# A bitwise search on VectorE: the count's start as a constant with one more column of gates, and a choice with one scalar and one tensor operand

## The chip, the cores and the metric

The kernel runs on one core of a Trainium2 chip. The metric is the device time of one execution in microseconds; the time before is the median of three runs. The profile is one further execution, recorded instruction by instruction. The engines are called PE (TensorE; PEld are its weight loads), DVE (VectorE), ACT (ScalarE), POOL (GpSimd) and SP (the queue that issues most transfers).

## What is computed

A transformer block with a mixture of experts, in float32, on 16 sequences of 256 tokens of width 256. The part that matters here is the routing, in which every expert takes the same number of tokens:

```python
shift = silu(t) @ W_ada.T + b_ada
h = _ln(x, ln1_g, ln1_b) + shift
# q, k, v of 16 heads of 64; layer norm on q and k; softmax attention
x = x + o @ Wout.T
tok = x.reshape(-1, d)                      # 4096 tokens
gate = softmax(tok @ Wgate.T, axis=-1)      # 8 experts
k_cap = bs // E                             # 512
vals, idx = top_k(gate.T, k_cap)            # each expert picks its 512 tokens
g = _ln(tok[idx], mlp_g, mlp_b)
y = (gelu(g @ fc1.T + b1) @ fc2.T + b2) * vals
tok = tok.at[idx].add(y)
```

## The kernel before

**Stages.** The sequences run through attention one after another, each split into steps (first norm, projections, scores, softmax, products, output projection, second norm, gates). Steps of neighbouring sequences are laid into each other. Up to line 1271 all engines follow a plan written out by hand: every step has a place (a number), the steps are sorted by place, and are issued in that order. So each engine has a fixed order of instructions, and an instruction that waits holds everything behind it on its engine. After that a loop over 15 jobs follows, in 16 slots each: matmuls of one expert, with the list, gather and transposes of the next job laid between.

**Two halves of the routing.** Each expert's 512 tokens are found in two halves of 256 (`CAPL`). The first search looks at the gates of the tokens that are ready (the others are held at -1.0 in `gate_of`), while the attention of the last sequence is still running. The second one runs inside the loop over jobs, and works on the gates that the first one left over. The jobs of the first half start as soon as their list is there.

**The first search** (`Routing`, steps placed by `SEARCH`, lines 437 to 453 and 1244) finds for every expert the bit pattern of the gate that 256 gates reach. `gT` holds the gates turned: 128 partitions of 256 gates, 16 partitions to an expert. There are 30 rounds, one bit each, and a round has four steps:

- `compare_less` (line 948) calls `compare` (898): one instruction on DVE compares 256 gates with the candidate `cand` and adds up how many reach it, starting the sum at `begin`, which is -255 on the first of an expert's 16 partitions and 0 on the others. The sum, `cnt`, comes out through a second small instruction that reads the accumulator.
- `count_over` (952): one matmul on PE adds the sums of an expert's 16 partitions, with the matrix `twice`, and leaves twice the surplus over 255 in PSUM (`pc`).
- `either` (958): two small operations on DVE make the two possible next candidates, `keep` and `drop`.
- `decide` (968): one operation on DVE makes the next candidate, the larger of `pc` and `drop`, but at most `keep`. A count enough gives `keep`, one too small gives `drop`.

After the rounds `masks` (977) marks the gates above and at the limit, and `scans`, `totals`, `place`, `turn_places`, `split` and `choose` give each chosen token its place. The lists of the jobs are then made with one-hot tiles (`onehot`, 1072) and matmuls (`list_matmul`, 1087); `gather` (1104) fetches the rows.

**The second search** takes two bits in a round, with three compares (`compare_three`, line 918), each with the candidate as its one scalar operand and without a start.

**Around the search** lie on PE the last sequence's projections (`pm`, line 631), transposes of q and k (`pq`, 673), scores (`sc`, 706), transposes of probabilities (`pp`, 742) and products (`po`, 760); on DVE their maxima (`nmax`, 713), sums of squares (`ss`, 648) and reciprocals (729); on ACT exponentials (722) and copies (640, 752, 770); on POOL powers (82) and scalings (664, 733).

**Preparation.** `make_others` (line 126), placed early in the plan, makes `high`, the first candidate, and `begin`. `gT` has one buffer in the pool `route`, which both searches use in turn; `reach`, the compares' element output that nobody reads, has two in the pool `bit`.

Of the kernel before, what the change touches and what calls it, by code (L numbers as in the profile page):

```python
# [9 lines left out]
F32 = mybir.dt.float32  # L10
I32 = mybir.dt.int32
BF16 = mybir.dt.bfloat16
AF = mybir.ActivationFunctionType
ALU = mybir.AluOpType
# [4 lines left out]
P = 128  # L19
# [13 lines left out]
CAPL = CAP // 2  # L33
# [10 lines left out]
def kernel(  # L44
# [14 lines left out]
    nc = tc.nc  # L59

    const = ctx.enter_context(tc.tile_pool(name="const", bufs=1))
    dram = ctx.enter_context(tc.tile_pool(name="dram", bufs=1, space=DRAM))
    route = ctx.enter_context(tc.tile_pool(name="route", bufs=1))
    bit = ctx.enter_context(tc.tile_pool(name="bit", bufs=2))
# [26 lines left out]
    vals = const.tile([P, E, NT, NV], BF16, name="vals")  # L91
    gate_of = const.tile([P, E, NT], F32, name="gate_of")
    high = const.tile([P, 1], I32, name="high")
    begin = const.tile([P, 1], F32, name="begin")
    first16 = const.tile([P, 1], I32, name="first16")

    def make_block():
# [28 lines left out]
    def make_others():  # L126
        nc.gpsimd.memset(gate_of, -1.0)
        nc.gpsimd.memset(high, 1 << 29)
        nc.gpsimd.iota(first16, pattern=[[0, 1]], base=0, channel_multiplier=1)
        nc.vector.tensor_scalar(first16, first16, 15, None, ALU.bitwise_and)  # L130
        nc.vector.tensor_scalar(begin, first16, 0.0, float(1 - CAPL), ALU.is_equal, ALU.mult)

    qgb = const.tile([P, 2], F32, name="qgb")
    sT = const.tile([P, DC, B], F32, name="sT")
# [341 lines left out]
    if True:  # L476
# [101 lines left out]
        class First:  # L578
# [22 lines left out]
            def evict(self):  # L601
                b = self.b
                hTs[b] = seq.tile([P, DC, N], F32, tag="hT", name=f"hT{b}")
                for c in range(DC):
                    nc.scalar.activation(
                        hTs[b][:, c, :], self.pt[:, c, :], AF.Identity,
                        bias=bias1[:, c, b : b + 1],
                        scale=vec[:, LN1_G + c : LN1_G + c + 1],
                    )
# [260 lines left out]
        class Routing:  # L870
# [11 lines left out]
                    nc.tensor.transpose(self.pt[:, r, :], gr[:, r, :], ident)  # L882

            def evict(self):
                self.gT = route.tile([P, 2 * P], F32, tag="gT", name="gT")
                pt = self.pt.rearrange("p r k -> p (r k)")
                if self.before is None:
                    nc.vector.tensor_copy(self.gT, pt)
                else:
                    nc.vector.scalar_tensor_tensor(  # L890
                        self.gT, self.before.chosen, -4.0, pt, ALU.mult, ALU.add
                    )
                self.cand = high

            def compare(self, n, start=None):
                reach = bit.tile([P, 2 * P], BF16, tag="reach", name="reach")
                self.cnt = bit.tile([P, 1], BF16, tag="cnt", name="cnt")  # L900
                nc.vector.tensor_scalar(
                    reach, self.gT, self.cand.bitcast(F32), start, ALU.is_ge, ALU.add,
                    accum_out=self.cnt,
                )


            def candidates(self, n):
# [10 lines left out]
            def compare_three(self, n):  # L918
                self.cnt = bit.tile([P, 3], BF16, tag="cnt3", name="cnt3")
                for k in range(3):  # L920
                    reach = bit.tile([P, 2 * P], BF16, tag="reach", name="reach")
                    nc.vector.tensor_scalar(
                        reach, self.gT, self.three[:, k : k + 1].bitcast(F32), None,
                        ALU.is_ge, ALU.add, accum_out=self.cnt[:, k : k + 1],
                    )

# [20 lines left out]

            def compare_less(self, n):

                self.compare(n, begin)  # L950

            def count_over(self, n):

# [14 lines left out]
            def decide(self, n):  # L968
                keep, drop = (new.bitcast(F32) for new in self.next)
                self.cand = bit.tile([P, 1], I32, tag="cand", name="cand")  # L970
                nc.vector.tensor_scalar(
                    self.cand.bitcast(F32), self.pc, drop, keep, ALU.max, ALU.min,
                )

# [257 lines left out]
        for k, f in enumerate((  # L1232
            make_block, make_twice, make_lanes, partial(make_vals, 0), partial(make_vals, 1),
            make_others,
        )):
            at([(4 + k / 8) * PERIOD], f)
# [156 lines left out]
```

## Time and profile before

| what | us |
|---|---|
| median of three runs (1182.08 to 1182.89) | 1182.83 |
| the profiled execution, its own time | 1182.07 |
| its span in the trace | 1180.30 |
| first search, from the first compare to the masks | 863.4 to 904.9 |
| first list's gather issued | 917.6 |
| busy over the span: PE, DVE, ACT, POOL | 1155.7, 755.3, 632.7, 593.2 |

All stamps are microseconds from the start of the span. A row of the groups view names line, engine, operation, what is written and read, the shapes and the count; behind the bar the busy time of all of them, then the mean duration of one in ns, then the engine's idle time before them and who ended it. The rows of the timeline give start, duration, engine, line and operation; in square brackets how long the engine had been idle and on whom it waited. "issue" is a wait with no cause that the profile shows. Operations of DVE that follow each other overlap a little, so the distance from one start to the next can be shorter than the duration. An operation with `accum_out` shows as `TENSOR_SCALAR_CACHE_REDUCE` and is followed by a `DVE_READ_ACCUMULATOR`.

### The profile page before, as it was taken

The page shows a single profiled execution, that of the slowest core. Times are in us where ns is not written, and L with a number is a line of the kernel's source. Part 1 is how long each engine was busy: PE and PEld are TensorE (multiplying, and loading weights), DVE is VectorE, ACT ScalarE, POOL GpSimd, SP SyncE. Part 2 cuts the span into 40 slices and gives each one's busy share as a digit, 9 for nine tenths or more (in the row PEclk, how much of TensorE's full clock was granted, in tenths as well). Part 3 has the DMA queues.
Part 4 walks back from the last instruction along what each step waited for, and adds up shares of the span by engine and source line. Part 5 has one row for each costly group of instructions (what it writes and reads, how often), then busy time and mean ns, then how long its engine had stood idle before and what let it go on. Part 6 is the DMA issues. An engine that isn't in the chain of part 4 may idle for free. (4 is left out here: it accounts for less than half of the span.)

```text
span 1180.3 us, 19683 instructions
## 1 busy us (share of the span) xinstructions
PE 1155.7 (98%) x6823; PEld 816.9 (69%) x6823; DVE 755.3 (64%) x2295; ACT 632.7 (54%) x1729; POOL 593.2 (50%) x821
## 2 busy tenths in 40 slices
PE   9999999999999999999999999999988899999996
PEld 5666666666666666666666666677745788888885
DVE  7656566657666566666666666665588578755540
ACT  4856656556565656565655565656466333233331
POOL 5846554556555555555555545464572233233332
PEclk9999999999999999999999999999999999999999
DMA  6000000000000000000000000000020465666661
GB/s 198 1 1 6 9 14 19 10 19 15 13 23 6 23 11 19 10 23 6 23 10 27 10 10 18 10 10 14 20 88 1 123 182 184 187 188 188 186 186 21
DMA packets 46739, 62.41 MB, mean 53 GB/s; under 512 B 3888, under 2 KB 39984, under 8 KB 46640
## 3 DMA queue, kind: packets, MB, share of 16 engines
q1 hardware_dynamic: 36864, 49.03, 12.5%
q0 software_dynamic: 6144, 8.39, 3.9%
q10 hardware_dynamic: 3632, 3.74, 1.0%
q8 instruction: 54, 0.88, 0.3%
q14 instruction: 45, 0.37, 0.1%
HBM read 48.56 MB, written 12.58 MB: 52 GB/s over the span
## 5 line engine op out<-in xcount | busy, mean ns | idle before, releaser
L631 PE MATMUL pm<-wq,hT 128*128 128x512 f32 x768 | 360.5, 599 | 1.2 <-ACT v L640 1.2
L733 POOL TENSOR_SCALAR pr<-pr,sums 128x256 f32<-128x256 f32 x512 | 236.5, 480 | 201.7 <-DVE sums L729 166.6
L722 ACT ACTIVATE pr<-sc,nmax 128x256 f32<-128x256 f32 x512 | 236.3, 477 | 125.1 <-DVE nmax L713 105.7
L82 POOL TENSOR_TENSOR ss<-ss,neghalf 128x8 f32<-128x8 f32 x128 | 211.6, 1655 | 172.9 <-DVE ss L652 162.5
L631 PEld LDWEIGHTS pm<-wq,hT 128*128 128x128 f32 x768 | 133.4, 190 | 120.3 <-issue 108.0
L713 DVE TENSOR_REDUCE nmax<-sc 128x2 f32<-128x512 f32 x256 | 166.4, 684 | 42.9 <-PE sc L706 42.9
L648 DVE TENSOR_REDUCE ss<-sq 128x8 f32<-128x512 f32 x128 | 87.3, 682 | 102.1 <-ACT sq L644 102.0
L742 PEld LDWEIGHTS pp<-ident,pr 128*128 128x128 f32 x1024 | 119.0, 141 | 47.3 <-issue 20.8
L742 PE MATMUL pp<-ident,pr 128*128 128x128 f32 x1024 | 138.4, 273 | 0.0
L644 ACT ACTIVATE sq<-pm 128x512 f32<-128x512 f32 x128 | 77.1, 603 | 99.0 <-PE pm L631 98.6
L706 PE MATMUL sc<-kT,qT 64*128 64x256 f32 x1024 | 129.7, 390 | 0.0
L760 PE MATMUL po<-prT,v 128*64 128x256 f32 x1024 | 124.6, 385 | 0.0
L706 PEld LDWEIGHTS sc<-kT,qT 64*128 64x128 f32 x1024 | 93.7, 186 | 38.2 <-issue 26.1
L784 PE MATMUL pw<-wo,oT 128*128 128x256 f32 x512 | 118.0, 383 | 0.0
L1135 PE MATMUL ph<-xT,w 128*128 128x256 f32 x512 | 117.8, 383 | 0.0
L1151 PE MATMUL py<-w,hid 128*128 128x256 f32 x512 | 116.3, 380 | 0.0
L1168 POOL DMA_INDIRECT out<-y,idx x32 | 51.2, 1601 | 123.9 <-DVE y L1162 70.7
L784 PEld LDWEIGHTS pw<-wo,oT 128*128 128x128 f32 x512 | 96.8, 192 | 18.9 <-issue 6.7
L722 ACT ACTIVATION_READ_ACCUMULATOR pr<-sc,nmax 128x1 f32 x512 | 106.3, 208 | 0.0
L1142 ACT ACTIVATE hid<-ph,vec 128x256 f32<-128x256 f32 x128 | 60.0, 473 | 83.5 <-PE ph L1135 78.3
L1151 PEld LDWEIGHTS py<-w,hid 128*128 128x128 f32 x512 | 95.6, 190 | 12.8
L1135 PEld LDWEIGHTS ph<-xT,w 128*128 128x128 f32 x512 | 95.3, 190 | 13.2 <-ACT xT L1123 0.4
(136 smaller groups left out, 1303.8 us busy)
## 6 DMA issues: line engine op xcount, KB each, us to landing
w<-in_fc2T SPq DMA_DIRECT2D x16, 1024.0 KB, 5.7
w<-in_fc1T SPq DMA_DIRECT2D x16, 1024.0 KB, 8.6
out<-tok SPq DMA_DIRECT2D x32, 128.0 KB, 1.7
xn_dram<-tn SPq DMA_DIRECT2D x32, 128.0 KB, 1.7
xs<-in_x SPq DMA_DIRECT2D x12, 256.0 KB, 2.8
b<-in_b2s SPq DMA_DIRECT2D x16, 128.0 KB, 8.7
wq<-in_wqkvT SPq DMA_DIRECT2D x3, 512.0 KB, 6.7
wq<-in_wqkvT ACTq DMA_DIRECT2D x3, 512.0 KB, 6.5
```

The costliest lines, as they stand in the source:

```text
L82: nc.gpsimd.tensor_tensor(dst, src, neghalf[:, : src.shape[1]], ALU.pow)
L631: nc.tensor.matmul(self.pm, hTs[self.b][:, c, bass.ts(self.t, P)], wq[:, c, bass.ts(self.g, GW)], start=(c == 0), stop=(c == DC - 1),)
L648: nc.vector.tensor_reduce(self.ss[:, 0, :], self.sq.rearrange("p (h d) -> p h d", d=HD), AX.X, ALU.add,)
L706: nc.tensor.matmul(self.sc[i, j][:, t, :], qTs[self.b][rows, hp, bass.ts(t, P)], kTs[self.b][rows, hp, :], start=True, stop=True,)
L713: nc.vector.tensor_reduce(self.nmax[i, j], self.sc[i, j], AX.X, ALU.max, negate=True)
L722: nc.scalar.activation(self.pr[i, j][:, t, :], self.sc[i, j][:, t, :], AF.Exp, bias=self.nmax[i, j][:, t : t + 1], scale=1.0, accum_out=se ...
L733: nc.gpsimd.tensor_scalar(self.pr[i, j][:, t, :], self.pr[i, j][:, t, :], self.sums[i][:, 1, j, t : t + 1], 1.0, ALU.mult, ALU.mult,)
L742: nc.tensor.transpose(self.pp[i, j][:, c, bass.ts(t, P)], self.pr[i, j][:, t, bass.ts(c, P)], ident,)
L760: nc.tensor.matmul(self.po[j * HD : (j + 1) * HD, i, :], vs[self.b][:, c, bass.ts(4 * self.d + 2 * i + j, HD)], self.prT[i, j][:, c, :], s ...
L784: nc.tensor.matmul(self.pw, oTs[self.b][:, hp, bass.ts(self.t, P)], wo[:, hp, :], start=(hp == 0), stop=(hp == HP - 1),)
L1135: nc.tensor.matmul(self.ph[f], self.w1[:, c, bass.ts(f, P)], self.xT[:, c, :], start=(c == 0), stop=(c == DC - 1),)
L1151: nc.tensor.matmul(self.py[i], self.hid[:, f, bass.ts(i, P)], self.w2[:, f, :], start=(f == 0), stop=(f == FC - 1),)
```

## The change

The column `begin` goes. Instead the tile of gates that the first search reads, `gates1`, has 257 columns, and its last one holds 3.0 on the first of an expert's 16 partitions and -1.0 on the others: a gate that always reaches the candidate, and one that never does. The sum starts at the constant -16 (`CAPL / 16`) on every partition, so that over an expert's 16 partitions it is 1 - 256 as before. `decide` takes `drop` as a scalar and `keep` as a tensor of one column. The second search uses the first 256 columns of a tile that is now one column wider, and `reach` is wider too. The order of the steps in the plan stays.

```diff
-    begin = const.tile([P, 1], F32, name="begin")
+    gates1 = route.tile([P, 2 * P + 1], F32, tag="gT", name="gates1")
...
-        nc.vector.tensor_scalar(begin, first16, 0.0, float(1 - CAPL), ALU.is_equal, ALU.mult)
+        nc.vector.tensor_scalar(
+            gates1[:, 2 * P :], first16, 0.5, 4.0, ALU.is_lt, ALU.mult
+        )
+        nc.vector.tensor_scalar_add(gates1[:, 2 * P :], gates1[:, 2 * P :], -1.0)
...
             def evict(self):
-                self.gT = route.tile([P, 2 * P], F32, tag="gT", name="gT")
                 pt = self.pt.rearrange("p r k -> p (r k)")
                 if self.before is None:
+                    self.gT = gates1[:, : 2 * P]
                     nc.vector.tensor_copy(self.gT, pt)
                 else:
+                    self.gT = route.tile([P, 2 * P + 1], F32, tag="gT", name="gT")[:, : 2 * P]
...
-            def compare(self, n, start=None):
-                reach = bit.tile([P, 2 * P], BF16, tag="reach", name="reach")
-                self.cnt = bit.tile([P, 1], BF16, tag="cnt", name="cnt")
-                nc.vector.tensor_scalar(
-                    reach, self.gT, self.cand.bitcast(F32), start, ALU.is_ge, ALU.add,
-                    accum_out=self.cnt,
-                )
...
             def compare_three(self, n):
-                    reach = bit.tile([P, 2 * P], BF16, tag="reach", name="reach")
+                    reach = bit.tile([P, 2 * P + 1], BF16, tag="reach", name="reach")
                     nc.vector.tensor_scalar(
-                        reach, self.gT, self.three[:, k : k + 1].bitcast(F32), None,
+                        reach[:, : 2 * P], self.gT, self.three[:, k : k + 1].bitcast(F32), None,
...
             def compare_less(self, n):
-                self.compare(n, begin)
+                reach = bit.tile([P, 2 * P + 1], BF16, tag="reach", name="reach")
+                self.cnt = bit.tile([P, 1], BF16, tag="cnt", name="cnt")
+                nc.vector.tensor_scalar(
+                    reach, gates1, self.cand.bitcast(F32), -CAPL / 16.0, ALU.is_ge, ALU.add,
+                    accum_out=self.cnt,
+                )
...
             def decide(self, n):
-                nc.vector.tensor_scalar(
+                nc.vector.scalar_tensor_tensor(
                     self.cand.bitcast(F32), self.pc, drop, keep, ALU.max, ALU.min,
                 )
```

## The prediction

> **What bounds the kernel now.** I read the page's busy times first, then the windows view cut at the borders of the first search, then the waits inside it, the groups by shape, and last the timeline of single rounds. The chain that ended last reaches back only over the final scatter (0.2% of the span) and helps nothing here.
>
> ```profile
> PE 1155.7 (98%) x6823; PEld 816.9 (69%) x6823; DVE 755.3 (64%) x2295; ACT 632.7 (54%) x1729; POOL 593.2 (50%) x821
> ```
> ```profile
> 862.00:905.00 43.00, 35.54 (x220) 21.47 (x222) 39.44 (x181) 29.76 (x86) 27.35 (x48) 1.00 0.03 8
> 905.00:925.00 20.00, 17.10 (x145) 13.11 (x141) 15.63 (x74) 8.61 (x25) 4.98 (x7) 0.91 0.07 21
> 925.00:1172.00 247.00, 243.96 (x1554) 213.28 (x1552) 144.45 (x778) 79.87 (x164) 80.04 (x66) 1.00 0.59 170
> ```
> The columns are length, then busy time of PE, PEld, DVE, ACT and POOL, granted clock, DMA share, GB/s. Over the whole span PE is the bound (98%). In the 43 us of the first search it is not: PE is busy 35.5, VectorE 39.4. The waits there name the cause:
>
> ```profile
> PE pc L956 <- DVE reach L901: 6.7, 10, 1.0
> ...
> PEld L956 <- DVE reach L901: 3.4, 5, 1.2
> ...
> DVE cand L971 <- PE pc L956: 0.3, 2, 0.2
> ```
> PE's order is fixed, so a count matmul that waits for VectorE's compare holds all matmuls behind it, and these belong to the last batch's attention. In the opposite direction VectorE waits hardly at all. So the search stage is set by VectorE and by the latency of the search's own loop. How the loop's latency adds up, from one round with nothing else between:
>
> ```profile
> 888.40 0.54 DVE L901 TENSOR_SCALAR_CACHE_REDUCE reach<-gT,cand,begin 128x256 bf16<-128x256 f32 x1
> ...
> 888.87 0.09 DVE L901 DVE_READ_ACCUMULATOR reach<-gT,cand,begin 128x1 bf16 x1
> ...
> 889.00 0.16 PE L956 MATMUL pc<-cnt,twice 128*128 128x1 bf16 x1 [0.39 <-DVE reach L901]
> ...
> 889.21 0.28 DVE L971 TENSOR_SCALAR cand<-pc,drop,keep 128x1 f32<-128x1 f32 x1
> ...
> 889.52 0.54 DVE L901 TENSOR_SCALAR_CACHE_REDUCE reach<-gT,cand,begin 128x256 bf16<-128x256 f32 x1
> ```
> Start to start: compare to accumulator read 0.47, to the count 0.13, to the decision 0.21, to the next compare 0.31; together 1.12 us. The search runs from 863.39 to the masks at 904.95, 41.6 us for 30 rounds: 1.12 is the round when bare, the rest are rounds into which VectorE's max, sums and scaling of attention (0.68 each) are laid. Both kinds contain one compare and one decision in sequence.
>
> **The change part by part.** The prices come from VectorE's groups by shape:
>
> ```profile
> L922 DVE TENSOR_SCALAR_CACHE_REDUCE reach<-gT,three 128x256 bf16<-128x256 f32 x45 | 19.2, 475 | 0.0
> L901 DVE TENSOR_SCALAR_CACHE_REDUCE reach<-gT,cand,begin 128x256 bf16<-128x256 f32 x29 | 15.6, 538 | 0.9
> ...
> L567 DVE TENSOR_SCALAR rs<-mv 128x1 f32<-128x1 f32 x64 | 9.8, 154 | 2.2
> L971 DVE TENSOR_SCALAR cand<-pc,drop,keep 128x1 f32<-128x1 f32 x30 | 8.3, 275 | 2.5 <-PE pc L956 0.3
> ...
> L944 DVE TENSOR_TENSOR cand<-cand,bits 128x1 int32<-128x1 int32 x13 | 2.1, 160 | 0.4
> ...
> L1004 DVE SCALAR_TENSOR_TENSOR place<-place,offset,mask 128x256 f32<-128x256 f32 x4 | 1.8, 483 | 0.1
> ...
> L1038 DVE SCALAR_TENSOR_TENSOR chosen<-places,one 128x256 f32<-128x256 f32 x1 | 0.4, 424 | 0.0
> ```
> Three pairs give one price for a per-partition scalar operand. Compare with two such (538) against one (475): 63 ns. One-column operation with two (275) against constants only (154): 60 each. Scalar-tensor-tensor with one (483) against none (424): 59.
>
> *Compare (L901).* It loses the scalar `begin` and gains a column. 475 ns is the same instruction with one scalar operand; 475 - 154 - 60 = 261 ns for 256 columns is 1.0 ns a column, so the new one is about 476, 62 ns less. No operation of 257 columns is in the trace. The cheap end is 475; at the dear end the odd width or the constant start eats the saving and it stays at 538. I take 476, because two rows (L922, and L981 at 476) carry the same form and one column is one element of a stream.
>
> *Decision (L971).* One scalar operand becomes a tensor operand. Nearest rows: tensor-tensor on one column 160, plus one scalar operand 60: 220. From L1004, 483 less 256 columns at 1.04 gives 217. The cheap end is 215, the dear end 275. I take 220: 55 ns less.
>
> The Trainium skill speaks against both. Its page "VectorE: DVE Perf Modes", section "The TRN2 errata — SBUF-src ops pay a fixed extra latency per instruction", prices an operation by where its source lies and by its columns, with no term for scalar operands, and its "Rules for kernel authors" advise lowering the number of operations, not fusing. The change keeps the number of operations in a round. By the page the sum is one cycle more per compare, an estimated 30 x 1 ns = 0.03 us lost: 1182.9. By the rows it is 30 x (62 + 55) = 3.5 us gained. The rows are three agreeing pairs from this kernel, so I go with them.
>
> *Preparation.* `begin` was one column operation of 154 ns at 282.3 us; now there are two, 0.15 us more. It hides under PE, 98% busy: VectorE has long idle spots in attention (102 us before the sums L648 alone). Bare it would cost 0.15 us.
>
> *Placement.* The order of instructions on all five engines is the same apart from that one. The build shifts every SBUF tile behind the bit pool by 64 bytes, and gives some of the small PSUM tiles another bank: in round 9 the count instead of the transposes before it waits for ACT's copy of v (done 875.50; the count ran 877.10), and in round 15 the projection behind the count waits for a copy done at 883.13 instead of the count (884.84). Both are over long before; nothing. No DMA is touched, and none is moved past.
>
> *What passes on.* A round in which VectorE is busy throughout gives up 117 ns like a bare one, unless PE's own matmuls between two counts take longer than the new round. I walked the timeline through 30 rounds, shifting each count to the later of the accumulator and the matmuls ahead of it. Eight scores (L706) between two counts take 1.16 to 1.18 us from count to count, eight transposes (L742) 1.06, four projections (L631) 1.83, sixteen products (L760) 1.97. A bare round falls to 1.00. The worst case is already late:
>
> ```profile
> 890.22 1.13 PE L706 MATMUL sc<-kT,qT 64*128 64x256 f32 x8
> ...
> 891.29 0.18 PE L956 MATMUL pc<-cnt,twice 128*128 128x1 bf16 x1
> ...
> 891.50 0.28 DVE L971 TENSOR_SCALAR cand<-pc,drop,keep 128x1 f32<-128x1 f32 x1 [0.18 <-PE pc L956]
> ```
> Lost: rounds 11 and 20 behind scores the whole 0.12 each, rounds 14 and 23 0.07 and 0.18 (where earlier gain runs into the same wall); rounds 19, 27, 28 behind eight transposes 0.17 together; rounds 16, 22, 25 behind projections and products 0.05. Sum 0.7. ACT and POOL are nearly full from 870 to 886, but their results are wanted later: POOL's scalings read at 886.7 end at 883.0. After the search the totals (906.41) stand behind sixteen products and come 0.1 late. So 3.5 - 0.7 - 0.1 = 2.7 us.
>
> The stage behind it is a chain from the search's result: places, one-hots (ACT's ten end at 916.9, and the list matmuls wait for them), list, gather at 917.6, then PE full to the end (244 of 247 us). The whole of it moves forward with the search. The profiled execution would go from 1182.07 (span 1180.30 and 1.77 around it) to 1179.4; the median of the runs, 0.76 above it, from 1182.83 to 1180.1.
>
> **The rivals.** *Scalar operands cost nothing inside the loop* (the page's view), or the 63 ns hide in the overlap of compare and accumulator read: 1182.8. Against it, masks L981 (0.48) reach their accumulator read after 0.40 us, the compare after 0.47. Chance 0.08.
>
> *Only one of the two savings comes, or PE and ACT hold more rounds than I counted*: the compare alone gives 1.5, the decision alone 1.3, half of the loss I found again 0.4: 1181.0 to 1181.9. For it speaks that 2.7 rests on margins of some 0.05 us between the loop and the matmuls. Chance 0.25.
>
> *The clock takes it back, and more.* From 914 to 917 PE is 43% busy (it waits for ACT's one-hots), and the next 3 us run at a granted clock of 0.50: sixteen projections take 5.25 us, where twelve at full clock took 2.86 (3.8 for sixteen), so the dip costs 1.4. The skill's "TensorE: Matmul & The Clock Gate", "Part 1: The HAM clock gate", says that the gate judges by a free-running window of about 3.4 us: with the search 2.7 us shorter the idle time falls elsewhere in it. One more such window takes 1.4, and from two more (2.9) on the kernel is slower; three would give 1180.1 + 4.3 = 1184.4. Against it, the gap itself is unchanged and PE has less idle time before it. Slower: chance 0.04.
>
> *The dip vanishes*: 1180.1 - 1.4 = 1178.7. Chance 0.06.
>
> **How the numbers follow.** My own case, 1180.1 within 0.5 either way, has 0.57. A measurement tells 0.2%, 2.4 us, from no change, that is below 1180.5 or above 1185.2. Three quarters of my own case and the vanished dip lie below 1180.5, and a little of the partial case: 0.43 + 0.06 + 0.04 = 0.53 faster. Slower by as much only if the clock case goes further than priced: 0.02. The rest, 0.45, is the same. The range runs from 1179.0 to 1182.0: it takes in my case and the partial one, and leaves out the vanished dip, the page's case and the clock, some 0.18.
>
> **What would show it.** Compare rows of 128x257 near 476 ns, decision rows (now scalar-tensor-tensor) near 220; bare rounds of 1.00 us; the stretch from the first compare to the masks 38.8 us instead of 41.6; PE's wait for `reach` down from 10 us in all to about 7; the gather 2.7 us earlier, and 925 to the end as long as before. It is wrong if the rows shrink and the search doesn't (then PE, ACT or POOL is the wall), if the search shrinks and the end doesn't move (the clock or the gather), or if the decision stays near 275.

## The result and the profile after

The changed kernel takes 1179.36 us (median of 13 runs, 1177.58 to 1182.5); the kernel before takes 1183.44 (13 runs, 1180.89 to 1184.55, the first three of them those that the forecast started from). The ratio of the two is 0.9971, with a 95% interval from 0.9962 to 0.998: the change gains some 3.4 us, by the interval 2.4 to 4.5. The profiled execution of the changed kernel took 1179.38 us, its span is 1177.6.

The windows view, at the same three stages as before. Columns: length, then busy time of PE, PEld, DVE, ACT and POOL, granted clock, DMA share, GB/s. The page's totals stand above it.

```profile
PE 1155.4 (98%) x6823; PEld 818.6 (70%) x6823; DVE 752.7 (64%) x2296; ACT 632.5 (54%) x1729; POOL 593.2 (50%) x821
```
```profile
862.00:902.30 40.30, 34.41 (x213) 20.67 (x212) 36.48 (x174) 29.49 (x90) 28.39 (x50) 1.00 0.07 25
902.30:922.30 20.00, 16.91 (x155) 12.84 (x154) 16.77 (x84) 9.88 (x29) 4.91 (x7) 1.00 0.07 21
922.30:1169.30 247.00, 244.24 (x1556) 213.58 (x1555) 144.63 (x778) 80.14 (x164) 80.41 (x66) 1.00 0.58 170
```
The second row of the kernel before had a granted clock of 0.91; here it is 1.00. The third row is what it was, and over the whole span PE is busy 98% as before. VectorE's groups in the search, by shape, and the waits there:

```profile
L950 DVE TENSOR_SCALAR_CACHE_REDUCE reach<-gates,cand 128x257 bf16<-128x257 f32 x29 | 14.0, 484 | 0.9
...
L974 DVE SCALAR_TENSOR_TENSOR cand<-pc,drop,keep 128x1 f32<-128x1 f32 x30 | 6.5, 216 | 3.0 <-PE pc L959 1.4
```
```profile
PE pc L959 <- DVE reach L950: 5.6, 9, 1.2
...
PEld L959 <- DVE reach L950: 1.5, 4, 0.6
DVE cand L974 <- PE pc L959: 1.4, 6, 0.3
```
The compare fell from 538 to 484 ns, the decision from 275 to 216. PE's waits for the compare (PE and PEld together) fell from 10.1 to 7.1 us, and VectorE's waits for the count rose from 0.3 to 1.4: the first comes of the gain, the second shows that PE's own matmuls now hold some of the counts back. A bare round is exactly as long as forecast, 1.00 us:

```profile
887.65 0.48 DVE L950 TENSOR_SCALAR_CACHE_REDUCE reach<-gates,cand 128x257 bf16<-128x257 f32 x1
...
888.65 0.48 DVE L950 TENSOR_SCALAR_CACHE_REDUCE reach<-gates,cand 128x257 bf16<-128x257 f32 x1
```

The two spans differ by 2.7 us, which is the number I forecast, but not by the sum that I forecast. I measured four stretches in both traces:

| stretch | before | after | difference |
|---|---|---|---|
| start of the span to the first compare | 863.39 | 864.92 | +1.53 |
| first compare to the masks | 41.56 | 39.11 | -2.45 |
| masks to the first expert matmul | 20.23 | 18.72 | -1.51 |
| first expert matmul to the end | 255.12 | 254.85 | -0.27 |

The first row has nothing to do with the change. PE's first weight loads differ already (the eight for `pa`, before and after):

```profile
5.05 1.09 PEld L512 LDWEIGHTS pa<-sT,wa 128*128 128x128 f32 x8 [0.34 <-issue]
```
```profile
4.82 1.78 PEld L517 LDWEIGHTS pa<-sT,wa 128*128 128x128 f32 x8
```
The first store of a finished token tile is then issued at 94.61 in one trace and at 96.15 in the other, and they stay 1.53 to 1.54 us apart up to 857. The 14 profiles of this study fall into two groups of seven: in one these loads take 0.97 to 1.20 us and the store is issued at 93.9 to 94.6, in the other they take 1.78 us and it is issued at 95.9 to 96.5. The changed kernel is in both (late here, early in its second profile, e0), and so are variants of the kernel before (e8 early, e9 late). The clock column reads 1.00 there in both traces, so what slows PE is not shown. The third row is the low clock of the kernel before, which the other trace does not have. So the agreement of the pair is in part luck, and the experiments below work on the second and the third row.

### The profile page after: what moved, and what is told of

Same layout as the page of the kernel before. It is cut to its first block, busy times and chain, and to the rows that moved or that the text cites. A ratio compares the mean times of both kernels' runs of the same rounds, so it can differ in the third digit from the quotient of the medians.

```text
span 1177.6 us, 19684 instructions
## 1 busy us (share of the span) xinstructions
PE 1155.4 (98%) x6823; PEld 818.6 (70%) x6823; DVE 752.7 (64%) x2296; ACT 632.5 (54%) x1729; POOL 593.2 (50%) x821
```

## The experiments

Two theories stood against each other for the part of the gain that was missing in the search (2.45 of 2.8 forecast): that PE's matmuls between two counts hold more rounds than I had counted, or that something else on VectorE became longer. For the third row the question was whether the change itself moves the clock.

**One half of the change alone.** e1 is the changed kernel with the old decision, e2 the old kernel with the new decision.

```
e1   -nc.vector.scalar_tensor_tensor(
     +nc.vector.tensor_scalar(
          self.cand.bitcast(F32), self.pc, drop, keep, ALU.max, ALU.min,
e2   the reverse, on the kernel before
```


> The new compare with the decision as before. If the search's loop sets the stage and both operations lie in it: compare rows 484 ns, decision rows 275; 30 x 0.054 = 1.6 us come off, about 0.4 of it lost again to PE and POOL, so first compare to masks 40.3 us (before 41.56, with both parts 39.11), time about 1.2 us under before. If the gain hangs on one operation alone: 39.1 here, and 41.6 in the run with the decision alone, or the other way round. If the time came from the start and the clock and not from the search: 41.6 here too.

> The new decision with the compare as before. By the theory of the loop: decision rows 217 ns, compare rows 538; 30 x 0.058 = 1.7 us come off and 0.4 are lost again: first compare to masks 40.2 us, time 1.3 us under before. By the rival, one operation alone: 41.6 or 39.1. By the rival of start and clock: 41.6.

Groups of e1, then of e2:

```profile
L950 DVE TENSOR_SCALAR_CACHE_REDUCE reach<-gates,cand 128x257 bf16<-128x257 f32 x29 | 14.0, 484 | 0.9
L974 DVE TENSOR_SCALAR cand<-pc,drop,keep 128x1 f32<-128x1 f32 x30 | 8.3, 276 | 2.7 <-PE pc L959 0.9
```
```profile
L901 DVE TENSOR_SCALAR_CACHE_REDUCE reach<-gT,cand,begin 128x256 bf16<-128x256 f32 x29 | 15.6, 538 | 0.9
L971 DVE SCALAR_TENSOR_TENSOR cand<-pc,drop,keep 128x1 f32<-128x1 f32 x30 | 6.5, 215 | 2.7 <-PE pc L956 0.7
```
The search took 40.27 us in e1 and 40.20 in e2, that is 1.29 and 1.36 less than before; together 2.65, where both at once gave 2.45. So each half gives about half, and they add up nearly. In time: e1 1182.12 (7 runs), ratio 0.9975 (0.9964 to 0.9987); e2 1181.92 (18 runs), ratio 0.9983 (0.9974 to 0.9991).

**The price of the compare's new form.** I had forecast 476 ns and 484 came. e3 lets the compare read 256 columns with the same constant start (it leaves out the column of gates that the change adds); e4 makes the tile 258 wide instead of 257, the last column a constant -1.

```
e3   -reach, gates1, self.cand.bitcast(F32), -CAPL / 16.0, ...
     +reach[:, : 2 * P], self.gT, self.cand.bitcast(F32), -CAPL / 16.0, ...
e4   -gates1 = route.tile([P, 2 * P + 1], ...)
     +gates1 = route.tile([P, 2 * P + 2], ...)      (reach and the later gT too)
     +nc.vector.memset(gates1[:, 2 * P + 1 :], -1.0)
```


> The changed kernel with the compare over 256 columns, but still with the constant start. It leaves out the extra column of gates, so every count is one lower. It asks why the compare took 484 ns where 476 were forecast. If the constant start costs it: 483. If the odd width does: 475.

> The changed kernel with 258 columns, the last one a gate of -1.0 everywhere that never reaches a candidate. If the odd width costs 8 ns: 477. If any column past 256 costs, or the constant does: 485 or a little more.

```profile
L950 DVE TENSOR_SCALAR_CACHE_REDUCE reach<-gates,cand 128x256 bf16<-128x256 f32 x29 | 13.9, 478 | 0.9
```
```profile
L951 DVE TENSOR_SCALAR_CACHE_REDUCE reach<-gates,cand 128x258 bf16<-128x258 f32 x29 | 14.0, 481 | 0.9
```
256 columns take 478, 258 take 481, 257 take 484. Against the 475 of the row that I had priced from, the constant start costs 3 ns at most, two columns more cost 3, and the odd width 4 or so on top of its column. Neither explanation alone covers the 8 ns. A bare round takes 1.00 us with each of the three widths and the search stays at 39.10 and 39.13 us, so the 8 ns are not what is missing; the one run of each took 1179.27 and 1177.2.

**The changed kernel again.**

> The changed kernel once more, to have it on the chip of the next three: 3.4 us under before (0.9971), give or take 1. Search stage (first compare to masks) 39.1 us again, since all in it is in fixed order; the scaling tn in round 7 again 1.17 us. If the 1.17 was chance, it is 0.4 to 0.7 and the stage 38.6.

On the chip of e5 to e7: 1178.64 us (5 runs), ratio 0.9963 (0.995 to 0.9976), the search again 39.11. But this profile has the low clock behind the search, 20.14 us from the masks to the first expert matmul. The low clock is therefore not something that the change removes: the same kernel has it in one execution and not in another.

**What is missing in the search.** From the start of one compare to the start of the next, the first six rounds gain 0.73 us together; in round 7 a part of it goes back. First the kernel before, then the changed one:

```profile
872.57 2.04 POOL L664 TENSOR_TENSOR qk<-qk,ss 128x512 f32<-128x512 f32 x2
...
874.08 0.68 DVE L573 TENSOR_SCALAR tn<-tok,mv,rs 128x256 f32<-128x256 f32 x1
```
```profile
873.79 2.04 POOL L669 TENSOR_TENSOR qk<-qk,ss 128x512 f32<-128x512 f32 x2
...
874.41 0.48 DVE L950 TENSOR_SCALAR_CACHE_REDUCE reach<-gates,cand 128x257 bf16<-128x257 f32 x1
...
874.82 1.17 DVE L578 TENSOR_SCALAR tn<-tok,mv,rs 128x256 f32<-128x256 f32 x1
```
`tn` is the scaling of a token tile for the later gather; its usual duration in this kernel is 0.40 (the median of 32). In both traces it ends 0.15 us after GpSimd's two scalings of `qk` (872.57 + 2.04 = 874.61, `tn` ends at 874.76; 873.79 + 2.04 = 875.83, `tn` ends at 875.99). VectorE comes to `tn` earlier against GpSimd, but is released with it, so 1.17 - 0.68 = 0.49 us of the 0.73 go back. In e1 and e2 the same instruction took 0.92 and 0.93, again ending just behind `qk`. Both traces have the pattern once more, ahead of the search; in the kernel before:

```profile
825.51 1.04 POOL L664 TENSOR_TENSOR qk<-qk,ss 128x512 f32<-128x512 f32 x1
825.58 1.12 DVE L573 TENSOR_SCALAR tn<-tok,mv,rs 128x256 f32<-128x256 f32 x1 [1.69 <-POOL rs L82]
```
`tn` ends there at 826.70, again 0.15 us behind the product (826.55). Beside GpSimd's other work, such as the scalings of `pr` (at 195.03), it keeps its 0.40. To test it I moved `tn` behind `qk`, in the changed kernel (e5) and in the kernel before (e8), by its place in the written order:

```
 tail=((914.489, 914.755, 921.894,
-       949.771,
+       999.900,
        917.193, 917.263, 917.528, 924.609), ...
```


> The changed kernel with the scaling tn of the last sequence but one moved from round 7 of the search to round 20, where GpSimd is idle and VectorE waits for PE anyway. If GpSimd's operation on qk held tn up (it ended 0.15 us after qk's end both before and after): tn 0.40 us, and the search stage 0.5 us shorter, 38.6. If tn was slow for another reason: it is still about 1 us in its new place and the stage stays at 39.1 or grows.

> The kernel before with only tn moved, as in e5. The move took 0.83 us off the changed kernel's search (39.11 to 38.28). If a part of the change's own gain had been lost to GpSimd's hold on tn (1.17 us after the change, 0.68 before it), the move brings less here, about 0.35, since tn loses 0.28 less: stage 41.2, and the change alone is then worth 2.9. If the hold has nothing to do with the change, the move brings the same 0.83 here: 40.7, and the change is worth 2.45 either way.

`tn` now runs in round 19 (not 20, as the expectation says) and takes 0.40 us in both. The search takes 38.28 us in e5, 0.83 less than in the changed kernel, more than the 0.77 by which `tn` itself shrank; in e8 it takes 41.16, only 0.40 less than before. So the move is worth 0.43 more to the changed kernel, and with `tn` out of the way the change's own gain in the search is 41.16 - 38.28 = 2.88 instead of 2.45. That shows the second theory. The time did not follow, against the expectation: e5 1180.24 (15 runs), ratio 0.9976 (0.9967 to 0.9985), no better than the changed kernel; e8 1181.32 (one run). The windows of e5 behind the search tell why for its profile:

```profile
912.00:914.00 2.00, 1.09 (x5) 0.83 (x6) 1.26 (x10) 1.08 (x4) 0.11 (x1) 0.61 0.03 8
914.00:916.00 2.00, 2.00 (x7) 1.55 (x6) 1.91 (x10) 0.00 (x0) 1.70 (x2) 0.50 0.09 20
916.00:918.00 2.00, 2.00 (x6) 1.63 (x5) 1.37 (x8) 0.00 (x0) 1.02 (x2) 0.50 0.57 176
```
PE waits for one-hots, then runs at half clock for over 4 us: 21.75 us from masks to expert matmuls, 3.0 more than with a full clock.

**Filling the gap.** If the low clock follows from PE's idle time there, dummy transposes between the list matmuls must prevent it. e6 puts four of them (0.63 us, results unused) ahead of each of the last five list matmuls of the first jobs; e9 does it in the kernel before; e7 is the changed kernel with both edits, e11 the kernel before with both.

```
+if a is jobs[0] and k == 5:
+    for t in range(5):
+        at([place + 0.001 * t], partial(fill, 4))
+        at([place + 0.001 * t], partial(a.list_matmul, w * k + t, w * k + t + 1))
+else:
     at([place], partial(a.list_matmul, w * k, w * k + w))
```


> The changed kernel with four transposes that nobody reads before each of the last five list matmuls, where PE waits for ACT's one-hots. If the low clock behind that gap explains the spread of single runs: granted clock 1.00 from 914 to 923 in the profile, the runs' lowest time as before, the highest 1.5 us lower. If the fills only stand in the way: 0.5 us slower in all runs, the spread unchanged. The search stage stays at 39.1.

> Both of the last two edits. If both theories hold: search stage 38.6, no low clock, 0.5 to 1 us under the changed kernel in the median. If the fills don't matter: 0.5 under it.

> The kernel before with only the fills in the gap. If the low clock behind the gap costs the kernel before as well: granted clock 1.00 from 914 to 924 in its profile, masks to the first expert matmul 18.8 us instead of 20.2, median about 1 us under before. If before has no such cost on the mean: the same as before.

> The kernel before with tn moved and the fills, as the counterpart to e7 and e12 on one chip: what is left between them is the change alone. By the theory of the loop the search stage is 41.2 and the time 2.9 us over that of e12; by the rival that half of the measured gain was the clock, under 2.0.

> The changed kernel with tn moved and the fills once more: search stage 38.28, masks to the first expert matmul 18.8, no low clock, median 4.5 us under before. If the fills work only by chance, one of its profile or e9's or e11's shows a clock under 1.00 there.

| run | search | masks to experts | median us (runs) | ratio (95%) |
|---|---|---|---|---|
| e6, change + fills | 39.11 | 18.78 | 1177.95 (5) | 0.9958 (0.9945 to 0.9971) |
| e7, change + both | 38.28 | 18.77 | 1178.75 (6) | 0.9965 (0.9953 to 0.9977) |
| e12, e7 again | 38.30 | 18.77 | 1178.36 (5) | 0.9959 (0.9945 to 0.9972) |
| e9, before + fills | 41.56 | 18.73 | 1182.22 (13) | 0.9996 (0.9988 to 1.0004) |
| e11, before + both | 41.16 | 18.72 | 1181.91 (13) | 0.9993 (0.9984 to 1.0001) |

The gap as the windows view of the kernel before and of e9 shows it:

```profile
914.00:917.00 3.00, 1.30 (x30) 0.96 (x27) 2.40 (x14) 2.71 (x9) 0.00 (x0) 0.95 0.02 5
```
```profile
915.70:918.70 3.00, 3.00 (x50) 2.95 (x47) 2.42 (x14) 2.72 (x9) 0.00 (x0) 1.00 0.02 5
```
Both windows start 9.05 us after the masks. With the fills PE is busy for all of the 3 us, and the clock behind the gap stays at 1.00 in all five profiles that have them; without them it fell in six of nine (before, e0, e1, e2, e5, e8; not in the changed kernel's first, e3, e4, where PE is busy for the same 1.30 or 1.31 us of the 3), each time at a cost of 1.4 to 3.0 us. The fills themselves cost under 0.1 (18.77 against 18.72). But in the runs they bring the kernel before nothing that can be measured (0.9996), though its profile without them lost 1.5. So either its unprofiled runs seldom have this low clock, or they lose the time at another place. e11 shows one such place. Its last stage, from the first expert matmul to the end, takes 256.95 us, against 255.73 in e2 and 254.85 to 255.32 in all others. The windows of e11 and then of e12, 5.0 us after their first expert matmul:

```profile
927.90:930.40 2.50, 0.95 (x7) 0.84 (x7) 2.50 (x16) 0.74 (x3) 0.00 (x0) 1.00 1.02 389
930.40:932.90 2.50, 2.50 (x8) 2.04 (x7) 2.47 (x16) 1.23 (x4) 0.00 (x0) 0.54 0.22 75
```
```profile
924.80:927.30 2.50, 1.25 (x8) 1.10 (x8) 2.50 (x16) 1.03 (x4) 0.00 (x0) 1.00 1.02 391
927.30:929.80 2.50, 2.50 (x14) 2.19 (x13) 2.47 (x16) 1.75 (x4) 0.00 (x0) 1.00 0.14 45
```
All profiles have this second gap, in which PE waits for the next gather; only in e11 the clock fell behind it. The wait itself is 1.17 to 1.40 us in the nine profiles with the new compare and 1.55 to 2.14 in the five with the old one. The gather is issued 0.44 us ahead of the first expert matmul in all of them, and lands later with the old compare. So some 0.3 us of the change's gain lie here (the -0.27 of the first pair's last row); what makes the gather land earlier is not shown.

The start and the two gaps, where PE's pace differs from one execution to the next, would account for runs of one kernel that lie 2 to 5 us apart. No unprofiled run shows its windows, but each has its mean granted clock on record. That is too coarse for one dip (the profile of the kernel before has one, and 0.997), but longer ones show: at 0.995 or under lie 33 of the 130 runs without the fills and one of the 42 with them; on one chip, 6 of 25 of the kernel before and one of 26 in e9 and e11. Of the kernel before it is 21 of 69 runs, 1184.1 us on the mean where the other 48 take 1183.1. So the fills keep the clock up in unprofiled runs too, but on these runs' numbers that is worth only some 0.3 us to the kernel before (an estimate: 21/69 of 1.0), which e9's interval can't show.

e11 and e12 are the cleanest pair for the change, as both have the fills and neither has `tn` in GpSimd's way: 38.30 against 41.16 in the search, 2.86 us, and medians of 1178.36 and 1181.91, 3.55 apart, on one chip. e6 and e12 have lower ratios than the changed kernel's (0.9971 and, in e0, 0.9963), but all four intervals overlap: that the fills or the moved `tn` make the changed kernel faster is not shown in time, only in its stages. Nor did the fills narrow the spread of the runs as expected: 1177.19 to 1179.74 in e6, 1177.19 to 1180.1 in e0.

## Why the prediction was right, and where it was not

The time forecast was 1180.1 us, 2.7 under the kernel before; 1179.36 came, 0.29% under it (0.20 to 0.38), which is 3.4 us.

*What sets the search stage:* right. The bare round fell from 1.12 to 1.00 us and the stage got shorter by 2.45, where 2.8 was forecast (41.6 to 38.8).

*The prices:* decision 216 ns for a forecast of 220; compare 484 for 476. Gross this is 30 x (54 + 59) ns = 3.4 us by the rows and 30 x 0.12 = 3.6 by the bare rounds, for a forecast of 3.5. "One column is one element of a stream" failed by 8 ns, for two small causes (e3, e4), and cost the rounds nothing. The rule that I set aside, the Trainium skill's "VectorE: DVE Perf Modes", "The TRN2 errata — SBUF-src ops pay a fixed extra latency per instruction", would have had the search stay as it was (30 ns longer); e1 and e2 each measure one scalar operand away, with the number of operations in a round unchanged, and each shortened the search, by 1.29 and 1.36 us.

*What PE's own matmuls hold back:* right in the sum, 0.7 us. Count to count behind eight scores is 1.17 us in the changed kernel, as long as before:

```profile
890.20 0.17 PE L959 MATMUL pc<-cnt,twice 128*128 128x1 bf16 x1
...
891.37 0.18 PE L959 MATMUL pc<-cnt,twice 128*128 128x1 bf16 x1
```
From the start of one compare to the start of the next, 20 of the 30 rounds got shorter by 0.12 us each. The other ten gave up less (e0 and e9 repeat every round of the two kernels within 0.01 us):

| rounds | lost, forecast | lost, measured |
|---|---|---|
| 11 and 20, behind scores | 0.24 | 0.22 |
| 14 and 23 | 0.25 | 0.23 |
| 19, 27, 28, behind transposes | 0.17 | 0.04 (19 alone) |
| 16, 22, 25, behind projections and products | 0.05 | 0.13 |
| 9 | 0 | 0.06 |
| 7 | 0 | 0.48 |

Without round 7 that is 0.68 us; in e5 and e8, with `tn` out of the way, all 30 rounds together lose 0.73. Some single rounds were priced wrong, and their errors cancel.

*The step that failed* is "a round in which VectorE is busy throughout gives up 117 ns like a bare one, unless PE's own matmuls ... take longer". In round 7 VectorE is busy throughout, and the round got longer, from 1.76 to 2.12 us: the busy time of `tn` is for the most part a wait for GpSimd that the trace shows as a longer instruction. I had checked POOL only for results that others want later. The sign was in the trace of before: `tn` took 0.68 there and 1.12 at 825.58, against 0.40 elsewhere, and ended behind `qk` both times. By e5 and e8 this cost the change 0.43 us in the search, 0.34 of it in round 7. The other 0.14 of that round is a wall of PE's that I had left out: with `tn` moved the round still gives up nothing (1.28 us in e8, 1.30 in e5), as its count stands behind four projections, 1.82 to 1.84 us from count to count in both. The decision of that round in e5 waits for it:

```profile
873.39 0.22 DVE L974 SCALAR_TENSOR_TENSOR cand<-pc,drop,keep 128x1 f32<-128x1 f32 x1 [0.37 <-PE pc L959]
```
Together 3.60 - 0.68 - 0.48 = 2.44 is the 2.45 that came, where I had 3.5 - 0.7 = 2.8.

*The stage behind moves whole:* right in its sense, but the pair of profiles can't show it to 0.1. The gather is issued 0.9 us earlier, which is the 2.45 of the search less the 1.54 by which this execution started later; I had forecast 2.7 without that. From the first expert matmul to the end I had forecast no difference; 254.85 came against 255.12, the shorter wait for the second gather.

*The preparation and the placement* cost nothing that can be seen: the two traces keep their distance of 1.53 to 1.54 us up to 857, past the added operation.

*The clock:* I named both its cases as rivals, taking it back (0.04) and the dip vanishing (0.06), as if the change decided between them. The runs show that neither belongs to the change: it has the dip in e0 and not in its first profile. That the span came out at -2.7 as forecast rests on this dip (-1.5) and the later start (+1.5) being equal, and on the last stage (-0.27) making up for what the search fell short of: luck, as far as the pair goes. Over many runs such things should mean out; the ratio's 3.4 us (2.4 to 4.5) takes in the 2.45 of the search and some 0.3 behind it, and whether the rest is clock or scatter stays open.

## What to carry to other kernels

In a loop of short dependent operations, count operands as well as operations: here two per-partition scalars less per round, with the same number of instructions, gave a tenth of the round. When work on one engine moves forward, look on it for instructions that take longer than their group's median and end together with another engine's: these are waits in disguise, and they give the gain back. Count what each round gives up, one by one: a right total can hide a wrong round. And before two profiles of a pair are compared, subtract what differs ahead of the first changed instruction and where the clock differs, or a right number may come out of a wrong sum.

## What was not expected of the hardware

A VectorE scaling of 128x256 f32 in SBUF took 0.40 us alone and 0.68, 0.92, 0.93 and 1.17 when it started ever earlier beside GpSimd's 2.04 us of 128x512 f32 products (1.12 beside a single one of 1.04), always ending about 0.15 us behind them. The compare on the same kind of data, which began at 874.41 beside the same products, kept its 0.48. The Trainium skill's "GPSIMD Engine Reference", "1. Specifications", has the two engines share SBUF interfaces, with contention for VectorE's instructions in a two-port mode or with two SBUF inputs; the runs fit that. `tn` has two per-partition scalars; less the 275 ns of a one-column operation with two, its 404 leave 129 ns for the columns, 0.5 ns each, where the compare's take 1.0 (an estimate from these rows). By this estimate the one that was held moves two columns at a time, and its 0.13 us of columns are about what it still takes once GpSimd is done. But only the move of `tn` tests the hold, and no run varies the instruction's mode.

A stretch of some 3 us in which PE was less than half busy was followed by a granted clock of about 0.5 in six of nine executions and by 1.00 in three, at a cost of 1.4 to 3.0 us where it fell, and one program (the changed kernel) had both; the Trainium skill's "TensorE: Matmul & The Clock Gate", "Part 1: The HAM clock gate", with its free-running window, would make it a matter of where the gap falls, which no run here shows. Five times four dummy transposes kept it at 1.00 in five of five.
